# Two half-tile loads of u from a doubled copy in DRAM, with the scan's partitions reordered

## The chip, the cores and the metric

The kernel runs on one core of one Trainium2 chip. The metric is the device time of one execution in microseconds, the median over runs. The profiled execution is one more run of the same program with the hardware profiler on. Its span is the time from the first to the last instruction of the program.

## The reference

The program computes four layers on x of shape (64, 11, 11, 128): 64 images of 121 tokens with 128 channels. Each layer is a mixer (called conv in the names) and then a feed-forward part (a mixture of experts in layer 0, a recurrent net in layers 1 and 2, a spectral filter in layer 3), both with a normalization ahead and a residual sum behind. The change lies in the mixer alone. Cut to what matters, with L = 256 positions (the inner channels are scanned over), D = 121 scan channels (the tokens) and 16 states n:

```python
xz = x @ in_proj_w.T                         # 128 -> 512 per token
xc, z = split(xz)                            # 256 each
xc = silu(conv1d(xc) + conv_b)               # per image: 121 tokens x 256
x_dbl = einsum('bkdl,kcd->bkcl', xs, x_proj_w)   # k = 0, 1: two directions
dts, Bs, Cs = split(x_dbl)                   # 8 ranks, 16 states, 16 states
delta = softplus(einsum('bkrl,kdr->bkdl', dts, dt_proj_w) + dt_proj_b)
dA  = exp(delta[..., None] * A)              # b k d l n
dBu = delta[..., None] * Bs * xs[..., None]  # = u * B, with u = delta * xs
h_l = dA_l * h_(l-1) + dBu_l                 # scan along l, for each b k d n
y   = einsum('bkdln,bknl->bkdl', h, Cs) + Ds * xs
y   = y[:, 0] + flip(y[:, 1])
out = (layernorm(y) * gelu(z)) @ out_proj_w.T
```

For each image b, direction k and scan channel d there is one row delta and one row u of 256 positions. The scan needs each of them once for every one of the 16 states.

## The kernel before

**Tiling.** A mixer works on 8 images at a time (CB = 8, so 8 groups c per layer) and on two directions k, which makes 16 passes m = 2c + k per layer and 64 in the program. The 128 partitions of a pass are 16 states times 8 images, partition = 8 * state + image. A pass walks over the 121 scan channels two at a time, in 61 steps (PAIRS). For every step:

- `rows` (L680, matmul at L686) spreads delta of a channel over the partitions: a 0/1 matrix `pick` (120 x 128, made in `made`, L146 to L150) picks the 8 images' delta, kept as three bf16 parts in the tile R, and repeats it for each state, into a PSUM tile da, five of which go round.
- `exps` (ACT, L699) makes exp(A * delta) in place, with A per partition.
- `scan` (DVE, L707) runs the recurrence over 2 x 256 positions, with da as the factor and ub as the addend, and writes one column of H or HX.
- `by_c` (PE, L728) multiplies blocks of H with C, held in Cz as one column per image (made from `own`, L170, by `own_c` on POOL).

**How u reaches the scan.** `steps` computes delta and u = delta * t for the next pass on PE, ACT and POOL, two images at a time, and `store` (L361 and L362) writes them to DRAM: delta to dD, u to uD of shape [group, direction, image, 128 channels, 256]. `load_u` (L659, the transfer at L663) brings u of four channels (a tile T, 31 tiles per pass, 1984 in all) to all 128 partitions: the source is the 8 images' rows of 4 x 256 floats, repeated for 16 states by a stride of zero. That makes 128 packets of 4 KB, 512 KB per tile. Six buffers (UB) go round. `times_b` (POOL, L675) then multiplies the tile by B in place, and two scans read it.

**What sets the order.** `run` writes every operation under a step number: the table AT (L87) has the step, within a pass or a group, at which each operation is put out, and each engine executes its own instructions in that order. Loads of u stand 10 steps ahead of their first scan (AT "lu"), the multiplication by B 5 steps ahead ("tb"). Loads of R (`load_r`, four quarters of a pass, two buffers) stand at "r0" to "r3". All DMAs of the mixer are issued by one queue, SP's, in order: a DMA that waits for its buffer holds back every DMA behind it. Each of them also waits for the DMA eight places ahead of it, since eight completion semaphores go round.

**Other lines that the change touches.** `load_bc` (L645) loads B and C of a pass to 128 partitions, one row of 1 KB each. `weights` loads A_logs (L135), repeated for the 8 images.

Of the kernel before, what the change touches and what calls it, by code (L numbers as in the profile page):

```python
# [8 lines left out]
F32 = mybir.dt.float32  # L9
# [31 lines left out]
def bcast(ap, n):  # L41

    return ap.unsqueeze(2).to_broadcast([ap.shape[0], ap.shape[1], n])
# [27 lines left out]
def act_tables(nc, which):  # L71
# [13 lines left out]
RING = 5  # L85
UB = 6
AT = {  # L87
    "x": -12.5, "st": -3, "mv": 3, "sc2": 6, "sc3": 8, "nm": 10, "tn": 13.5, "td": 15.5, "tn2": 17.5,
    "td2": 19.5, "cv": 20, "cve": 49, "silu": 52, "p0": 53, "pa0": 3.75, "s0": 66, "b0": 66, "ba0": 7.875,
    "p1": 100, "pa1": 2.25, "s1": 109, "b1": 111, "ba1": 7.5, "u": 4, "d0": 1, "r": 3, "d1": 5, "l": 6.5,  # L90
    "d2": 7, "dst": 12.5, "bc": 54, "bca": 3, "sk": 99, "ska": 2.5, "y0": 15.5, "y1": 35, "y2": 57.5, "y3": 82,
    "k0": 27, "k1": 44.5, "k2": 66.5, "k3": 89, "ka": 2, "ks": 2.5, "km": 4.5, "k2s": 6.5, "k3s": 9, "kn": 11,
    "kg": 13, "xa": 28.5, "xb": 66, "g0": 38, "z0": 77, "g1": 81.5, "z1": 109, "ga": 5, "za": 3.5, "gt": 117.5,
    "gta": 2, "ge": 126.5, "cz": 8, "cza": 3.75, "lbc": -18, "lu": 10, "tb": 5, "ys": 8, "ysa": 1, "ysh": 8,
    "r0": -10, "r1": 2, "r2": 23, "r3": 37,
}


class Conv:
# [9 lines left out]
    def weights(self, setup, fixed, ps):  # L109
        cx, nc, a = self.cx, self.nc, self.cx.a  # L110
        p = f"L{self.l}_conv_"

        def load(pool, name, shape, src):
            t = pool.tile(shape, F32, name=name)
            nc.sync.dma_start(t, src)
            return t

        in_x = load(setup, "in_x", [128, 2, C], a[p + "in_x"].rearrange("(q p) c -> p q c", p=128))
        conv_wT = load(
            setup, "conv_wT", [128, 3, 2, L], a[p + "conv_wT"].rearrange("j (q p) o -> p j q o", p=128)  # L120
        )
        x_dt = load(setup, "x_dt", [8, 2, D], a[p + "x_dt"])
        dt_wT = load(setup, "dt_wT", [8, 2, D], a[p + "dt_wT"])
        self.Ds = fixed.tile([128, 2], F32, name="Ds")
        nc.vector.memset(self.Ds, 0.0)
        nc.sync.dma_start(self.Ds[:D], a[p + "Ds"])
        self.in_zT = load(fixed, "in_zT", [C, L], a[p + "in_zT"])
        self.conv_b = load(fixed, "conv_b", [1, L], a[p + "conv_b"])
        self.x_bc = load(fixed, "x_bc", [D, 4 * NS], a[p + "x_bc"])
        self.norm = load(fixed, "norm", [D, 2], a[p + "norm"])  # L130
        self.out_wT = load(fixed, "out_wT", [128, 2, C], a[p + "out_wT"].rearrange("(q p) c -> p q c", p=128))

        self.A = fixed.tile([128, 2, D], F32, name="A")
        for k in range(2):
            nc.sync.dma_start(self.A[:, k, :], a[p + "A_logs"][k].unsqueeze(1).to_broadcast([NS, CB, D]))  # L135
        return lambda: self.made(setup, fixed, ps, in_x, conv_wT, x_dt, dt_wT)

    def made(self, setup, fixed, ps, in_x, conv_wT, x_dt, dt_wT):
        cx, nc, a = self.cx, self.nc, self.cx.a
        p = f"L{self.l}_conv_"  # L140
        af = self.A.rearrange("p k d -> p (k d)")
        nc.scalar.activation(af, af, AF.Exp)
        nc.vector.tensor_scalar_mul(af, af, -1.0)


        pick = setup.tile([5 * 24, 5, CB], F32, name="pick")  # L146
        nc.vector.reduce_sum(pick, cx.ident[:120, :120].rearrange("p (a s b) -> p a b s", s=3, b=CB), axis=AX.X)
        self.pick = fixed.tile([5 * 24, 5, NS, CB], BF16, name="pick16")
        for i in range(5):
            nc.vector.tensor_copy(self.pick[:, i], pick[:, i, :].unsqueeze(1).to_broadcast([120, NS, CB]))  # L150

        self.w_conv = fixed.tile([C, 3, L], F32, name="w_conv")
        for j in range(3):
            pw = ps.tile([C, L], F32, name="pw", tag="mm")
            for q in range(2):
                nc.tensor.matmul(pw, in_x[:, q, :], conv_wT[:, j, q, :], start=(q == 0), stop=(q == 1))
            nc.scalar.copy(self.w_conv[:, j, :], pw)


        self.w_dt = fixed.tile([D + 1, 2, 128], F32, name="w_dt")  # L160
        nc.vector.memset(self.w_dt, 0.0)
        nc.sync.dma_start(self.w_dt[D : D + 1, :, :D], a[p + "dt_b"].unsqueeze(0))
        for k in range(2):
            pw = ps.tile([D, D], F32, name="pdt", tag="mm")
            nc.tensor.matmul(pw, x_dt[:, k, :], dt_wT[:, k, :], start=True, stop=True)
            nc.scalar.copy(self.w_dt[:D, k, :D], pw)
        self.ones = fixed.tile([1, 128], F32, name="ones")
        nc.vector.memset(self.ones, 1.0)

        self.own = fixed.tile([128, CB], F32, name="own")  # L170
        nc.vector.reduce_sum(self.own, cx.ident.rearrange("p (n b) -> p b n", b=CB), axis=AX.X)

    def buffers(self, fixed, work, ps_f, dram):
        cx, nc, NC = self.cx, self.nc, self.NC
# [12 lines left out]
            nc.gpsimd.memset(x[:, :, 0 : D + 2 : D + 1], 0.0)  # L187
        self.skip = [fixed.tile([D, CB, L], F32, name=f"skip{i}") for i in range(2)]
        self.yst = fixed.tile([128, 64, D], F32, name="yst")
        self.uD = dram.tile([NC, 2, CB, 128, L], F32, name="uD")  # L190
        self.dD = dram.tile([NC, 2, 128, 3, CB, L], BF16, name="dD")
        self.bcD = dram.tile([NC, 4 * NS, CB, L], F32, name="bcD")
        self.yD = dram.tile([NC, L, CB * D], F32, name="yD")
# [99 lines left out]
    def steps(self, c, k, at=None):  # L293
# [10 lines left out]
        for b in range(0, CB, 2):  # L304
# [54 lines left out]

            def store(b=b, s=s):  # L360
                nc.sync.dma_start(self.dD[c, k, :, :, b : b + 2, :].rearrange("d s b l -> d s (b l)"), s["d"])  # L361
                nc.sync.dma_start(  # L362
                    self.uD[c, k, b : b + 2].rearrange("b d l -> d b l"), s["u"].rearrange("p (b l) -> p b l", l=L)
                )

            i = b // 2
            fs = (u, first, rest, second, less, third, store)
# [272 lines left out]
    def load_bc(self, m):  # L640
        c, k = m // 2, m % 2
        for name, at in (("Bt", 0), ("Cp", NS)):
            x = self.work.tile([128, L], F32, name=name, bufs=2)
            r0 = 2 * NS * k + at
            self.nc.sync.dma_start(x, self.bcD[c, r0 : r0 + NS].rearrange("r b l -> (r b) l"))  # L645
            self.bc[m, name] = x

    def own_c(self, m, u):
# [9 lines left out]
    def load_u(self, T):  # L658
        m, i = divmod(T, TILES)  # L659
        n = min(4, D - 4 * i)  # L660
        x = self.work.tile([128, 4, L], F32, name="ub", bufs=UB)
        self.ub[T] = x
        self.nc.sync.dma_start(  # L663
            x[:, :n, :].rearrange("p d l -> p (d l)"),
            self.uD[m // 2, m % 2, :, 4 * i : 4 * i + n, :]
            .rearrange("b d l -> b (d l)")
            .unsqueeze(0)
            .to_broadcast([NS, CB, n * L]),
        )

    def times_b(self, T):
        m, i = divmod(T, TILES)
# [7 lines left out]
    def rows(self, g):  # L680

        m, p = divmod(g, PAIRS)
        for j in range(self.channels(p)):
# [1 line left out]
            n = 24 if d == D - 1 else 120  # L685
            self.nc.tensor.matmul(  # L686
                self.da[g % RING][:, j, 1:],
                self.pick[:n, d % 5].rearrange("p n b -> p (n b)"),
                self.R[m, d // 35][:n, d % 35 // 5, 1:],
                start=True,  # L690
                stop=True,
# [803 lines left out]
```

## Time and profile before

| what | value |
|---|---|
| median of 3 runs | 7753.25 us (7753.02 to 7753.61) |
| the profiled execution | 7752.68 us, span 7750.9 us |
| busy, PE / DVE / ACT / POOL | 6041.0 / 5659.8 / 5449.4 / 5293.3 us |
| POOL, u times B (L675) | 4557.2 us in 1984 instructions of 2323 ns |
| DVE, scans (L707) | 2391.8 + 2130.4 us |
| ACT, exponentials (L699) | 3291.7 us |
| loads of u (ub<-uD) | 1920 of 512 KB and 64 of 128 KB |
| stores of u (uD<-u) | 256 of 256 KB |
| moved by DMA | 1536.54 MB in 905471 packets |

The profile has one line per engine with its busy share in 40 slices of the span, the same for the 16 DMA engines, a list of groups of instructions (busy time, mean of one, idle time ahead of them and what ended it), a list of waits, and the chain of work that ended last. The four mixers can be read off the DMA line: four stretches near 9, with the feed-forward parts between and behind them. A matmul's busy time is modelled, so PE's 78% is not a measure of how full PE is. The shares are averages over stages with different limits, so each stretch is also asked for by itself.

### The profile page before, as it was taken

The page shows a single profiled execution, that of the slowest core. Times are in us where ns is not written, and L with a number is a line of the kernel's source. Part 1 is how long each engine was busy: PE and PEld are TensorE (multiplying, and loading weights), DVE is VectorE, ACT ScalarE, POOL GpSimd, SP SyncE. Part 2 cuts the span into 40 slices and gives each one's busy share as a digit, 9 for nine tenths or more (in the row PEclk, how much of TensorE's full clock was granted, in tenths as well). Part 3 has the DMA queues.
Part 4 walks back from the last instruction along what each step waited for, and adds up shares of the span by engine and source line. Part 5 has one row for each costly group of instructions (what it writes and reads, how often), then busy time and mean ns, then how long its engine had stood idle before and what let it go on. Part 6 is the DMA issues. An engine that isn't in the chain of part 4 may idle for free. (4 is left out here: it accounts for less than half of the span.)

```text
span 7750.9 us, 208787 instructions
## 1 busy us (share of the span) xinstructions
PE 6041.0 (78%) x84334; PEld 3448.5 (44%) x84334; DVE 5659.8 (73%) x7849; ACT 5449.4 (70%) x12343; POOL 5293.3 (68%) x2659
## 2 busy tenths in 40 slices
PE   6788778776788877766788888767678887758999
PEld 3444444465344444444344444434344444434445
DVE  5888888844788888962788888871788888872201
ACT  7888888733888888853788888862788888852200
POOL 6798999812888888931888888940888898960000
PEclk8888898777898989875889989875788888879999
DMA  7899999856899999942899999951899999971111
GB/s 181 227 247 243 245 246 243 215 167 170 221 241 249 246 240 244 247 110 75 220 241 244 246 248 243 243 140 37 217 236 243 243 245 241 245 184 46 35 39 36
DMA packets 905471, 1536.54 MB, mean 198 GB/s; under 512 B 136840, under 2 KB 617442, under 8 KB 904503
## 3 DMA queue, kind: packets, MB, share of 16 engines
q1 hardware_dynamic: 903223, 1521.09, 76.3%
q8 instruction: 662, 10.85, 0.6%
q14 instruction: 306, 2.51, 0.1%
q10 hardware_dynamic: 1280, 2.10, 0.1%
HBM read 1265.98 MB, written 256.97 MB: 196 GB/s over the span
## 5 line engine op out<-in xcount | busy, mean ns | idle before, releaser
L675 POOL TENSOR_TENSOR ub<-ub,Bt 128x1024 f32<-128x1024 f32 (+1 forms) x1984 | 4557.2, 2323 | 589.7 <-DMA ub<-uD 447.1
L699 ACT ACTIVATE da<-da,A 128x255 f32<-128x255 f32 x7744 | 3291.7, 451 | 696.1 <-PE da L686 612.0
L707 DVE TENSOR_TENSOR_SCAN H<-da,ub 128x512 f32<-128x512 f32 x2048 | 2391.8, 1208 | 354.4 <-POOL ub L675 183.9
L707 DVE TENSOR_TENSOR_SCAN HX<-da,ub 128x512 f32<-128x512 f32 (+1 forms) x1856 | 2130.4, 1190 | 318.5 <-POOL ub L675 160.1
L686 PE MATMUL da<-R,pick 120*128 120x255 bf16 x7744 | 1658.9, 305 | 546.0 <-DVE H L707 277.3
L686 PEld LDWEIGHTS <-pick 120*128 120x128 bf16 x7744 | 662.9, 103 | 1494.6 <-issue 1054.9
L728 PE MATMUL yb<-H,Cz 128*16 128x64 f32 x32768 | 782.2, 236 | 187.7 <-ACT yst L745 107.7
L728 PE MATMUL yb<-HX,Cz 128*16 128x64 f32 x32768 | 813.4, 237 | 122.6 <-DVE HX L707 62.7
L728 PEld LDWEIGHTS yb<-HX,Cz 128*16 128x16 f32 x32768 | 531.3, 105 | 641.9 <-issue 338.1
L728 PEld LDWEIGHTS yb<-H,Cz 128*16 128x16 f32 x32768 | 540.9, 103 | 584.0 <-issue 313.3
L263 PE MATMUL pc<-w_conv,xnT 128*121 128x256 f32 x1344 | 458.7, 433 | 27.4 <-ACT d L358 18.6
L184 POOL MEMSET t<- 128x2048 f32 x4 | 7.2, 1805 | 599.6 <-PE px L1221 211.8
L313 PE MATMUL pd<-t,w_dt 122*128 122x512 f32 x480 | 317.6, 749 | 101.7 <-ACT t L274 55.1
L745 ACT COPY yst<-yb 128x512 f32<-128x512 f32 (+2 forms) x640 | 334.9, 551 | 83.9 <-DMA yD<-yst 70.2
L743 DVE TENSOR_TENSOR yst<-yst,yb 128x512 f32<-128x512 f32 (+2 forms) x640 | 337.1, 543 | 73.7 <-PE yb L728 73.2
L340 PE MATMUL pr<-sp,ident 128*128 128x512 f32 x480 | 302.7, 717 | 80.0 <-ACT sp L301 75.0
L333 POOL TENSOR_TENSOR u<-sp,t 128x512 f32<-128x512 f32 x240 | 307.6, 1282 | 33.9 <-DMA uD<-u 32.8
L1294 DVE COPY U<-pu 128x488 f32<-128x488 f32 x128 | 85.4, 667 | 282.5 <-PE pu L1327 282.5
L1296 ACT COPY U<-pu 128x488 f32<-128x488 f32 x128 | 72.9, 570 | 308.7 <-PE pu L1327 308.7
L652 POOL TENSOR_TENSOR Cz<-Cp,own 128x512 f32<-128x512 f32 x256 | 275.5, 1076 | 0.0
L329 ACT CAST d<-sp 128x512 bf16<-128x512 f32 x240 | 148.6, 619 | 172.1 <-DMA dD<-d 171.9
L263 PEld LDWEIGHTS pc<-w_conv,xnT 128*121 128x121 f32 x1344 | 211.7, 194 | 94.9 <-ACT d L358 25.0
(237 smaller groups left out, 7243.8 us busy)
## 6 DMA issues: line engine op xcount, KB each, us to landing
ub<-uD SPq DMA_DIRECT2D x1920, 512.0 KB
dD<-d SPq DMA_DIRECT2D x256, 384.0 KB
R<-dD SPq DMA_DIRECT2D x192, 420.0 KB
uD<-u SPq DMA_DIRECT2D x256, 256.0 KB
yD<-yst SPq DMA_DIRECT2D x512, 60.5 KB
y<-yD SPq DMA_DIRECT2D x112, 242.0 KB
bcD<-bc SPq DMA_DIRECT2D x128, 128.0 KB
w1g<-in_L_ffn_weight_dram SPq DMA_DIRECT2D x16, 1024.0 KB
```

The source lines that it names most:

```text
L263: nc.tensor.matmul(pc, lhs, rhs, start=(j == 0), stop=(j == taps - 1))
L313: nc.tensor.matmul(s["p"], self.w_dt[:, k, :], tb[: D + 1], start=True, stop=True)
L333: nc.gpsimd.tensor_mul(s["u"], s["sp"], tb)
L340: nc.tensor.matmul(s["pr"], self.cx.ident, s["sp"], start=True, stop=False, skip_group_check=True)
L652: self.nc.gpsimd.tensor_mul(self.Cz[u], C.unsqueeze(2).to_broadcast([128, 64, CB]), self.own.unsqueeze(1).to_broadcast([128, 64, CB]),)
L675: self.nc.gpsimd.tensor_mul(x, x, self.bc[m, "Bt"].unsqueeze(1).to_broadcast([128, n, L]))
L686: self.nc.tensor.matmul(self.da[g % RING][:, j, 1:], self.pick[:n, d % 5].rearrange("p n b -> p (n b)"), self.R[m, d // 35][:n, d % 35 // ...
L699: self.nc.scalar.activation(x, x, AF.Exp, scale=self.A[:, m % 2, d : d + 1])
L707: self.nc.vector.tensor_tensor_scan(self.H[dq % 2][:, :n, p - DQ[dq][0]], self.da[g % RING].rearrange("p j l -> p (j l)")[:, :n], x.rearra ...
L728: self.nc.tensor.matmul(self.yb[32 * q : 32 * q + 16, slot % 8, :, :, :w], self.Cz[slot // 8][:, place % 64 : place % 64 + 2, :].rearrange ...
L743: nc.vector.tensor_add(dst, dst, src)
L745: nc.scalar.copy(dst, src)
```

## The change

u is stored twice in DRAM: uD gets a dimension of 2 behind the image, and `store` issues two DMAs with the same data. A tile of u is then loaded by two transfers of 256 KB, one for partitions 0 to 63 and one for 64 to 127. The source of each is 16 rows (image, copy), each repeated for four partitions that follow one another, where it was 8 rows, all repeated 16 times. So that this fits, the partitions stand in another order: half of the states, image, state within the half (partition = 64 * half + 8 * image + state). `pick`, `own`, A and the loads of B and C follow that order; B, C and A are loaded in two halves. Besides that, 18 entries of AT are moved, most of them by half a step to two steps; "r1" goes from 2 to -6, "gt" from 117.5 to 114.5.

```diff
--- before.py
+++ after.py
@@ -85,14 +85,14 @@
 RING = 5
 UB = 6
 AT = {
-    "x": -12.5, "st": -3, "mv": 3, "sc2": 6, "sc3": 8, "nm": 10, "tn": 13.5, "td": 15.5, "tn2": 17.5,
-    "td2": 19.5, "cv": 20, "cve": 49, "silu": 52, "p0": 53, "pa0": 3.75, "s0": 66, "b0": 66, "ba0": 7.875,
-    "p1": 100, "pa1": 2.25, "s1": 109, "b1": 111, "ba1": 7.5, "u": 4, "d0": 1, "r": 3, "d1": 5, "l": 6.5,
-    "d2": 7, "dst": 12.5, "bc": 54, "bca": 3, "sk": 99, "ska": 2.5, "y0": 15.5, "y1": 35, "y2": 57.5, "y3": 82,
-    "k0": 27, "k1": 44.5, "k2": 66.5, "k3": 89, "ka": 2, "ks": 2.5, "km": 4.5, "k2s": 6.5, "k3s": 9, "kn": 11,
-    "kg": 13, "xa": 28.5, "xb": 66, "g0": 38, "z0": 77, "g1": 81.5, "z1": 109, "ga": 5, "za": 3.5, "gt": 117.5,
-    "gta": 2, "ge": 126.5, "cz": 8, "cza": 3.75, "lbc": -18, "lu": 10, "tb": 5, "ys": 8, "ysa": 1, "ysh": 8,
-    "r0": -10, "r1": 2, "r2": 23, "r3": 37,
+    "x": -12.5, "st": -3, "mv": 3, "sc2": 6, "sc3": 8, "nm": 10, "tn": 12.5, "td": 14.5, "tn2": 17.5, "td2": 19.5,
+    "cv": 20, "cve": 49, "silu": 51, "p0": 53, "pa0": 3.75, "s0": 66, "b0": 66, "ba0": 7.875, "p1": 99.5,
+    "pa1": 2.25, "s1": 109, "b1": 111, "ba1": 7.5, "u": 3, "d0": 1, "r": 3, "d1": 4, "l": 6.5, "d2": 7, "dst": 12.5,
+    "bc": 54, "bca": 3, "sk": 99, "ska": 2.5, "y0": 17, "y1": 35, "y2": 56.5, "y3": 82.5, "k0": 26.5, "k1": 44.5,
+    "k2": 65.5, "k3": 89.5, "ka": 2, "ks": 2.5, "km": 4.5, "k2s": 6, "k3s": 9, "kn": 11, "kg": 13, "xa": 30.5,
+    "xb": 66, "g0": 36, "z0": 77, "g1": 81.5, "z1": 109, "ga": 5, "za": 3.5, "gt": 114.5, "gta": 2, "ge": 124.5,
+    "cz": 8, "cza": 3.75, "lbc": -18, "lu": 10, "tb": 5, "ys": 8, "ysa": 1, "ysh": 8, "r0": -10, "r1": -6, "r2": 23,
+    "r3": 37,
 }
 
 
@@ -132,7 +132,9 @@
 
         self.A = fixed.tile([128, 2, D], F32, name="A")
         for k in range(2):
-            nc.sync.dma_start(self.A[:, k, :], a[p + "A_logs"][k].unsqueeze(1).to_broadcast([NS, CB, D]))
+            for h in range(2):
+                A = a[p + "A_logs"][k, 8 * h : 8 * h + 8].unsqueeze(0).to_broadcast([CB, 8, D])
+                nc.sync.dma_start(self.A[64 * h : 64 * h + 64, k, :], A)
         return lambda: self.made(setup, fixed, ps, in_x, conv_wT, x_dt, dt_wT)
 
     def made(self, setup, fixed, ps, in_x, conv_wT, x_dt, dt_wT):
@@ -145,9 +147,10 @@
 
         pick = setup.tile([5 * 24, 5, CB], F32, name="pick")
         nc.vector.reduce_sum(pick, cx.ident[:120, :120].rearrange("p (a s b) -> p a b s", s=3, b=CB), axis=AX.X)
-        self.pick = fixed.tile([5 * 24, 5, NS, CB], BF16, name="pick16")
+        self.pick = fixed.tile([5 * 24, 5, 2, CB, 8], BF16, name="pick16")
         for i in range(5):
-            nc.vector.tensor_copy(self.pick[:, i], pick[:, i, :].unsqueeze(1).to_broadcast([120, NS, CB]))
+            for h in range(2):
+                nc.vector.tensor_copy(self.pick[:, i, h], bcast(pick[:, i, :], 8))
 
         self.w_conv = fixed.tile([C, 3, L], F32, name="w_conv")
         for j in range(3):
@@ -168,7 +171,9 @@
         nc.vector.memset(self.ones, 1.0)
 
         self.own = fixed.tile([128, CB], F32, name="own")
-        nc.vector.reduce_sum(self.own, cx.ident.rearrange("p (n b) -> p b n", b=CB), axis=AX.X)
+        own = setup.tile([128, 2, CB], F32, name="own2")
+        nc.vector.reduce_sum(own, cx.ident.rearrange("p (h b n) -> p h b n", h=2, b=CB), axis=AX.X)
+        nc.vector.tensor_add(self.own, own[:, 0], own[:, 1])
 
     def buffers(self, fixed, work, ps_f, dram):
         cx, nc, NC = self.cx, self.nc, self.NC
@@ -187,7 +192,7 @@
             nc.gpsimd.memset(x[:, :, 0 : D + 2 : D + 1], 0.0)
         self.skip = [fixed.tile([D, CB, L], F32, name=f"skip{i}") for i in range(2)]
         self.yst = fixed.tile([128, 64, D], F32, name="yst")
-        self.uD = dram.tile([NC, 2, CB, 128, L], F32, name="uD")
+        self.uD = dram.tile([NC, 2, CB, 2, 128, L], F32, name="uD")
         self.dD = dram.tile([NC, 2, 128, 3, CB, L], BF16, name="dD")
         self.bcD = dram.tile([NC, 4 * NS, CB, L], F32, name="bcD")
         self.yD = dram.tile([NC, L, CB * D], F32, name="yD")
@@ -359,9 +364,11 @@
 
             def store(b=b, s=s):
                 nc.sync.dma_start(self.dD[c, k, :, :, b : b + 2, :].rearrange("d s b l -> d s (b l)"), s["d"])
-                nc.sync.dma_start(
-                    self.uD[c, k, b : b + 2].rearrange("b d l -> d b l"), s["u"].rearrange("p (b l) -> p b l", l=L)
-                )
+                for i in range(2):
+                    nc.sync.dma_start(
+                        self.uD[c, k, b : b + 2, i].rearrange("b d l -> d b l"),
+                        s["u"].rearrange("p (b l) -> p b l", l=L),
+                    )
 
             i = b // 2
             fs = (u, first, rest, second, less, third, store)
@@ -642,7 +649,9 @@
         for name, at in (("Bt", 0), ("Cp", NS)):
             x = self.work.tile([128, L], F32, name=name, bufs=2)
             r0 = 2 * NS * k + at
-            self.nc.sync.dma_start(x, self.bcD[c, r0 : r0 + NS].rearrange("r b l -> (r b) l"))
+            for h in range(2):
+                rows = self.bcD[c, r0 + 8 * h : r0 + 8 * h + 8]
+                self.nc.sync.dma_start(x[64 * h : 64 * h + 64], rows.rearrange("r b l -> b r l"))
             self.bc[m, name] = x
 
     def own_c(self, m, u):
@@ -660,13 +669,12 @@
         n = min(4, D - 4 * i)
         x = self.work.tile([128, 4, L], F32, name="ub", bufs=UB)
         self.ub[T] = x
-        self.nc.sync.dma_start(
-            x[:, :n, :].rearrange("p d l -> p (d l)"),
-            self.uD[m // 2, m % 2, :, 4 * i : 4 * i + n, :]
-            .rearrange("b d l -> b (d l)")
-            .unsqueeze(0)
-            .to_broadcast([NS, CB, n * L]),
-        )
+        rows = self.uD[m // 2, m % 2, :, :, 4 * i : 4 * i + n, :].rearrange("b i d l -> (b i) (d l)")
+        for h in range(2):
+            self.nc.sync.dma_start(
+                x[64 * h : 64 * h + 64, :n, :].rearrange("p d l -> p (d l)"),
+                rows.unsqueeze(1).to_broadcast([2 * CB, 4, n * L]),
+            )
 
     def times_b(self, T):
         m, i = divmod(T, TILES)
@@ -685,7 +693,7 @@
             n = 24 if d == D - 1 else 120
             self.nc.tensor.matmul(
                 self.da[g % RING][:, j, 1:],
-                self.pick[:n, d % 5].rearrange("p n b -> p (n b)"),
+                self.pick[:n, d % 5].rearrange("p h b n -> p (h b n)"),
                 self.R[m, d // 35][:n, d % 35 // 5, 1:],
                 start=True,
                 stop=True,
```

## The prediction

> **What bounds the kernel now.** I read the page's slices first, then its chain and groups.
>
> ```profile
> DMA  7899999856899999942899999951899999971111
> GB/s 181 227 247 243 245 246 243 215 167 170 221 241 249 246 240 244 247 110 75 220 241 244 246 248 243 243 140 37 217 236 243 243 245 241 245 184 46 35 39 36
> ...
> PE 17%; ACT 7%; DMA 7%; DVE 5%; issue 4%; POOL 3%; SPq 0%; DVEq 0%; ACTq 0%; POOLq 0%
> ...
> L675 POOL TENSOR_TENSOR ub<-ub,Bt 128x1024 f32<-128x1024 f32 (+1 forms) x1984 | 4557.2, 2323 | 589.7 <-DMA ub<-uD 447.1
> ...
> ub<-uD SPq DMA_DIRECT2D x1920, 512.0 KB
> ```
>
> In the mixers the DMA line stands at 9 while the rate sticks near 245 GB/s. POOL, the engine that receives u, was idle 589.7 us ahead of L675, 447.1 of it for the loads of u. Stretches of the third and fourth mixer, a stretch with loads of u alone, and one with plain loads of expert weights:
>
> ```profile
> 3700.00:5150.00 1450.00, 1145.33 (x19660) 643.77 (x19658) 1264.65 (x1554) 1209.89 (x2731) 1267.29 (x628) 0.87 0.94 236
> 5450.00:6900.00 1450.00, 1133.57 (x19279) 635.73 (x19276) 1265.53 (x1558) 1216.81 (x2753) 1282.31 (x638) 0.86 0.94 238
> ...
> 68.00:70.00 2.00, 0.00 (x0) 0.00 (x0) 0.47 (x1) 1.78 (x5) 2.00 (x2) 0.50 1.05 252
> ...
> 1685.00:1687.00 2.00, 2.00 (x11) 2.00 (x11) 0.00 (x0) 0.00 (x0) 0.00 (x0) 0.50 1.05 396
> ```
>
> The columns are PE, PEld, DVE, ACT and POOL busy, clock, DMA share, GB/s. In a mixer POOL is busy 88%, DVE 87%, ACT 84%, and DMA 94%: four resources are nearly full, DMA the most. Yet with all DMA engines busy the loads of u move 252 GB/s and the weights 396. In the trace's packet records a 4 KB packet takes 255 ns on average (255,077 of them) and 159 ns when nothing hinders it (the median of the stores around 5371 us, and 23% of all). The third view is of waits:
>
> ```profile
> POOL ub L675 <- DMA ub<-uD: 447.1, 313, 14.9
> ...
> PEld L686 <- DMA R<-dD: 87.0, 42, 9.9
> ```
>
> and SP's own:
>
> ```profile
> SPq L663 <- DVE H L707: 1730.4, 826, 7.5
> SPq L663 <- DVE HX L707: 1342.3, 635, 6.1
> ```
>
> SP spends 3073 us waiting for scans to free a buffer of u. It has time to issue more.
>
> [...] Before has one transfer of 64 partitions, the store bcD<-bc: its 2 KB packets take 140 ns around 42 us, where the weights' take 84 in the median. [...] this speaks against the change. [...] The load of 121 rows around 1574 us has 11 packets in flight at once[...].
>
> **Why a packet takes 255 ns.** Two causes fit. [...] Shared rows: all 16 engines read the same 4 KB of DRAM at once. Transfers with own rows and blocks of neighbouring partitions show the first alone: the first load of R (62.7 to 65 us) has 36.8 ns against an undisturbed 27 (1.36 times), the loads HX<-mid around 1575 us 201 against 159 (1.27). Loads of u by themselves (65.5 to 76 us) have 269 (1.69). The difference, 1.69 against about 1.31, I put down to shared rows, which the change ends. The first load of conv_b, one row of 1 KB to 121 partitions, shows it too: 61 ns on average against 44 for its undisturbed packets.
>
> **The change part by part.**
>
> Loads of u: 245,760 packets of 4 KB remain. [...] I take 1.31 times 159 = 208. That is 47 ns by 15,360 packets per engine: -722 us of DMA time.
>
> Second store of u: 256 DMAs, 16 packets of 1 KB per engine, 52.3 ns each in the mixers: +214 us. Its issue (580 to 620 ns) is 256 x 0.6 = 154 us of SP.
>
> More DMAs: the two programs have 4207 and 6583, 2376 more (1984 half loads, 256 stores, 128 for B and C, 8 for A). Each ends in a completion packet per engine, 13 ns: +31 us. SP's issue of a load of u is 515 ns, and the 64-row bcD<-bc is no cheaper (480 to 520), so the half loads cost SP 1984 x 0.515 = 1022 us. The 3073 us of buffer waits cover it. Uncovered, a tile would come half a microsecond later, in 313 waits 160 us; but the first half takes 4 x 208 ns = 0.8 us to move, so the second is in its queue in time. Nothing.
>
> Each DMA still waits for the one eight places ahead, which now is four tiles instead of eight. SP waited 34.0 us for that in all; tripled it is 100, under the same cover. [...]
>
> DMA sum: -722 + 214 + 31 = -477 us, of 5617 us that the packets take in the four mixers (16 engines, 6140 us). The share falls from 0.94 to about 0.86.
>
> Moved "r1": the second load of R stands 8 steps earlier, at -6, while the last rows of the pass before still read its buffer until step -4. SP stands for two steps of 1.57 us (6140 us over 3904 steps), 64 times, with loads of u queued behind. Those have five steps (7.9 us) until POOL wants them, and need 3.9 (0.5 to issue, 1.3 to the first packet of a load into idle queues, 2.1 to move). Cost between -50 (R's 87 us of waits shrink) and +190 (cover gone); I take 0. The other entries move the same instructions by at most 3 steps: 0, between -40 and +40. PE, POOL and SP keep their instructions otherwise; DVE and SP have a few more in the setup, behind the feed-forward parts, and 1.3 us ahead of the first mixer.
>
> From DMA time to span: the free share of DMA goes from 6% to 14%, and I take half of POOL's 447.1 us away: -224. POOL's other waits at L675 are 143 of 590, a quarter; they take back 56 as DVE, ACT and PE come due next. R's waits fall in the same moments and are not counted. 7752.7 - 224 + 56 + 1 = 7586; the median stands 0.6 us above the profiled execution, so 7587.
>
> **The rivals.**
>
> Nothing is relieved, and the second store is in the way (the other sign). Place: the queues ahead of POOL's L675, behind each store of u. For it: the bcD<-bc packets at 1.67[...]. Against: R and HX<-mid at 1.27 to 1.36. Price: +245 us of DMA time on a share of 0.94; 50% to 95% reaches the end: 7875 to 7985. It decides where a packet falls by less than 245 / 15,360 = 16 ns, so stays above 239.
>
> Engines in step: [...] packets at 266 to 302. DMA +414 to +967 us, against 370 us free: 8000 to 8650. For it: bcD again; against: in the mixers the loads come ragged, and 23% of the packets already run undisturbed.
>
> Full relief: packets near 170, DMA no longer binds. Against more than that: POOL at 88% would go to 93%. All 447 less a quarter: -335, 7418.
>
> The change may not do what it says: relief of just 16 ns, and gain and store cancel: 7738 to 7768.
>
> **How the numbers follow.** Part relief, 7440 to 7720: 0.50. Full relief: 0.07. Cancelled: 0.07. Second store in the way: 0.27. In step: 0.09. What can be told from no change is 0.2%, 15.5 us. Faster 0.57, same 0.07, slower 0.36. The forecast is the likeliest, 7587, with its own range 7440 to 7720. The range 7400 to 7980 leaves out the in-step case and the edges of two others, under 0.2.
>
> **What would show it.** 4 KB packets near 208 ns; DMA share near 0.86 in the same stretches of a mixer; POOL's wait for ub<-uD near 220 us; R's waits below 153 (87.0 for PEld, 66.0 for PE); written to HBM 67 MB more than 256.97. Wrong if the packet stays above 239, if SP waits for DMAs rather than scans, or if POOL's gain reappears as waits of DVE for ACT.

## The result, and the profile after

| | before | after |
|---|---|---|
| median | 7753.14 us (7744.28 to 7753.61, 4 runs) | 7871.21 us (7863.89 to 7878.85, 4 runs) |
| ratio | | 1.0155, 95% interval 1.0138 to 1.0173 |
| profiled execution, its span | 7752.68, 7750.9 us | 7863.89, 7862.1 us |

The changed kernel is 1.55% slower. The forecast was 7587, faster by 2.1%: its sign is wrong. The time lies in the stated range, just below the band of the rival in which the second store is in the way (7875 to 7985).

The experiments below were each compared with runs of the kernel before made beside them (medians of 7765 to 7769 us), so their ratios do not follow from 7753.

From the page of the changed kernel: the DMA slices, what went through memory, POOL's product and the two issues.

```profile
DMA  7899999956899999942899999960899999971111
GB/s 187 230 251 253 252 253 251 229 151 174 230 257 254 254 248 253 252 119 69 224 250 250 251 251 249 250 163 22 220 245 251 253 252 257 250 198 47 35 39 36
...
HBM read 1265.98 MB, written 324.08 MB: 202 GB/s over the span
...
L683 POOL TENSOR_TENSOR ub<-ub,Bt 128x1024 f32<-128x1024 f32 (+1 forms) x1984 | 4560.0, 2323 | 701.6 <-DMA ub<-uD 580.3
...
ub<-uD SPq DMA_DIRECT2D x3840, 256.0 KB
uD<-u SPq DMA_DIRECT2D x512, 256.0 KB
```

The 67 MB more that are written are the second copy of u. DMA moves some 8 GB/s more in the mixers, and its slices still stand at 9. The same two stretches as before (PE, PEld, DVE, ACT and POOL busy, clock, DMA share, GB/s):

```profile
3700.00:5150.00 1450.00, 1120.96 (x18542) 619.00 (x18556) 1225.25 (x1505) 1193.04 (x2690) 1240.61 (x616) 0.85 0.94 246
5450.00:6900.00 1450.00, 1105.53 (x17951) 615.87 (x17964) 1200.24 (x1495) 1173.55 (x2630) 1202.03 (x602) 0.87 0.91 241
```

The share is 0.94 and 0.91 where 0.86 was forecast, at a rate 4% and 1% higher. POOL does less in the same 1450 us (616 and 602 pieces of work where it did 628 and 638). The waits of those who receive u and R:

```profile
POOL ub L683 <- DMA ub<-uD: 580.3, 354, 19.9
...
PEld L694 <- DMA R<-dD: 107.9, 44, 11.8
...
PE da L694 <- DMA R<-dD: 75.9, 27, 10.2
```

All three grew: POOL's from 447.1 us, R's from 87.0 and 66.0. The last of these, and SP's wait for DMAs at the loads of u, in the kernel before:

```profile
PE da L686 <- DMA R<-dD: 66.0, 28, 8.3
...
SPq L663 <- DMA ub<-uD: 34.0, 46, 2.4
```

SP's own waits at the loads of u (L674) in the changed kernel:

```profile
SPq L674 <- DVE H L715: 613.5, 372, 6.6
SPq L674 <- DVE HX L715: 529.7, 393, 6.8
...
SPq L674 <- DMA ub<-uD: 339.8, 721, 1.7
...
SPq L674 <- DMA R<-dD: 115.4, 76, 3.5
```

SP waited 3073 us for scans before and waits 1143 now. The DMA landings in the traces of both kernels fall on eight semaphores, and SP's waits for the DMA eight places ahead, a load of u or of R, rose from 34.0 us to 455 here. The prediction had named as a sign of being wrong "if SP waits for DMAs rather than scans"; this goes that way, though scans are still the larger part.

For the comparisons below I worked out one table from the trace's packet records and issues. It takes, in each of the four mixers, the stretch from the last issue of the 20th tile's load to the first of the 477th's, of 496, and adds the four up. "Busy" is the time of all packets divided by 16 engines, "idle" is the rest, both in us. The packet column is the mean of the packets of 4096 bytes that start in the stretches. "Late" is the mean time from the end of the scan that frees a tile's buffer to the end of the last issue of that tile's load.

| kernel | transfers per tile | ratio to before | stretch | busy | idle | 4 KB packet, ns | late, us |
|---|---|---|---|---|---|---|---|
| before | 1 | 1 | 5440 | 5137 | 303 | 255.6 | 1.37 |
| after | 2 | 1.0155 | 5536 | 5251 | 284 | 247.9 | 3.37 |
| e1_store | 1 | 1.0100 | 5516 | 5294 | 223 | 253.5 | 1.76 |
| h1_halves | 2 | 1.0077 | 5494 | 5126 | 367 | 251.8 | 3.00 |
| e2_oldat | 2 | 1.0199 | 5588 | 5305 | 283 | 252.2 | 3.39 |
| e4_one | 1 | 1.0045 | 5458 | 5141 | 317 | 246.2 | 1.58 |
| s3_row | 2 | 1.0055 | 5490 | 5201 | 289 | 258.1 | 2.13 |
| s4_row | 3 | 1.0280 | 5661 | 5256 | 405 | 262.2 | 3.82 |
| s1_tiny | 2 | 1.0084 | 5513 | 5220 | 293 | 257.2 | 2.24 |
| s2_tiny | 3 | 1.0392 | 5769 | 5330 | 438 | 262.2 | 4.45 |
| v1_middle | 3 | 1.0345 | 5699 | 4867 | 831 | 238.3 | 5.77 |

In the last column the s-kernels are measured at the load of u, with their extra transfers behind it.

### The profile page after: what moved, and what is told of

The parts are those of the page before. It is cut to its first block, busy times and chain, and to the rows that moved or that the text cites. A ratio compares the mean times of both kernels' runs of the same rounds, so it can differ in the third digit from the quotient of the medians.

```text
span 7862.1 us, 214588 instructions
## 1 busy us (share of the span) xinstructions
PE 6067.6 (77%) x84282; PEld 3442.9 (44%) x84334; DVE 5671.2 (72%) x7873; ACT 5442.1 (69%) x12343; POOL 5293.6 (67%) x2659
## 5 line engine op out<-in xcount | busy, mean ns | idle before, releaser
L683 POOL TENSOR_TENSOR ub<-ub,Bt 128x1024 f32<-128x1024 f32 (+1 forms) x1984 | 4560.0, 2323 | 701.6 <-DMA ub<-uD 580.3
```

The lines of the kernel that those rows point to most:

```text
L683: self.nc.gpsimd.tensor_mul(x, x, self.bc[m, "Bt"].unsqueeze(1).to_broadcast([128, n, L]))
```

## The experiments

### Which partitions, or shared rows

A program of loads alone, none of the mixers: 30 loads one after the other in each of six forms, from a DRAM tensor laid out like uD (the comments number the forms). "Shared" are 8 rows (4 in form 6), all repeated 16 times, "own" are 16 rows, each repeated for 4 or 8 partitions that follow one another.

```diff
+    def before(t, i):                       # form 1: 8 rows, repeated 16 times
+        nc.sync.dma_start(t, shared(i, 128, 8))
+    def halves(t, i):                       # form 2: 16 own rows, twice 64 partitions
+        for h in range(2):
+            nc.sync.dma_start(t[64 * h : 64 * h + 64], own(i, 4))
+    def one(t, i):                          # form 3: 16 own rows, 128 partitions
+        nc.sync.dma_start(t, own(i, 8))
+    def middle(t, i):                       # form 4
+        nc.sync.dma_start(t[32:96], own(i, 4))
+    def low(t, i):                          # form 5
+        nc.sync.dma_start(t[0:64], own(i, 4))
+    def middle_shared(t, i):                # form 6: 4 rows, repeated 16 times
+        nc.sync.dma_start(t[32:96], shared(i, 64, 4))
```

> No mixer is in this kernel: it copies x to the output and then loads 4 KB rows of a small DRAM buffer in six forms, 30 buffers each, nothing else moving. The forms: (a) as before, 16 copies of 8 shared rows; (b) as after, two halves of 16 own rows by 4 partitions; (c) one transfer of 16 own rows by 8 partitions; (d) 16 own rows by 4 partitions to partitions 32 to 95 alone; (e) the same to partitions 0 to 63 alone; (f) partitions 32 to 95 with 16 copies of 4 shared rows. Theory of shared rows (the prediction's): the mean 4 KB packet is near 269 ns in (a), near 208 in (b) and (c), and (f) is slower than (d). [...] (a), (b) and (c) are all between 255 and 285 ns, (d) is near 159 and (e) near 300 although both have own rows, and (f) equals (d).

The windows of the six forms in that order (the last two columns are DMA share and GB/s):

```profile
64.00:107.00 43.00, 3.23 (x21) 0.00 (x0) 1.00 1.03 251
133.00:179.00 46.00, 3.25 (x22) 0.00 (x0) 1.00 1.04 243
203.00:246.00 43.00, 2.99 (x20) 0.00 (x0) 1.00 1.03 235
270.00:287.00 17.00, 5.96 (x42) 0.00 (x0) 1.00 0.94 331
300.00:327.00 27.00, 3.07 (x21) 0.00 (x0) 1.00 1.03 204
342.00:359.00 17.00, 6.34 (x44) 0.00 (x0) 1.00 0.96 342
```

In these windows packets of 4 KB take 267 ns in the form of before, 275 in that of the change and 285 in one transfer of own rows: rows of their own bring nothing. Sixty-four partitions from 32 to 95 take 183.3 ns with own rows and 181.9 with shared ones, with a median of 159, the undisturbed time. From 0 to 63 it is 327, with a median of 326. So which partitions are written decides between these (331 and 342 GB/s against 204), and not whether rows are shared. The prediction's step on 255 ns had put the length down to shared rows; here it does not come from them. Why the packets of the three forms with 128 partitions take 267 to 285 ns, no run shows.

### The second store alone

```diff
-        self.uD = dram.tile([NC, 2, CB, 128, L], F32, name="uD")
+        self.uD = dram.tile([NC, 2, CB, 2, 128, L], F32, name="uD")
...
-                nc.sync.dma_start(
-                    self.uD[c, k, b : b + 2].rearrange("b d l -> d b l"), s["u"].rearrange("p (b l) -> p b l", l=L)
-                )
+                for i in range(2):
+                    nc.sync.dma_start(
+                        self.uD[c, k, b : b + 2, i].rearrange("b d l -> d b l"),
+                        s["u"].rearrange("p (b l) -> p b l", l=L),
+                    )
```

> The kernel before with u stored twice and the second copy never read; everything else as before. Theory of the second store: the 214 us of DMA time that it adds reach the end by more than half, 7860 to 7960 us. Theory that the halves cost it (their issues, completions and the waits on eight semaphores): the store is hidden, 7750 to 7790 us.

Measured: 7844.55 us, 1.0100 (1.0080 to 1.0119), nearer to the first theory and just under its band. In the table it adds 157 us of busy time: packets of 1 to 2 KB, which hold the stores of u, add 177 for 92% of the added stores, and those of 4 KB give back 28. Idle time takes up 80, and the stretch is 76 us longer. POOL's wait, and the third mixer:

```profile
POOL ub L677 <- DMA ub<-uD: 540.5, 341, 15.8
```

```profile
3700.00:5150.00 1450.00, 1122.39 (x18813) 625.98 (x18813) 1240.85 (x1531) 1207.58 (x2725) 1259.10 (x627) 0.86 0.96 249
```

DMA goes to a share of 0.96, in this window and over the four stretches (5294 of 5516 us), and of the engine time added beside the loads of u about half is paid. That supports the first view of the prediction: DMA is what binds. The 256 stores also take 256 issues and places in SP's queue, which this run does not separate; by the cost of transfers of a single number further below (1984 for 0.55%) they would be worth some 6 of the 77 us, an estimate that takes a store to hold its place no longer than such a transfer does.

### The halves without the store, and one transfer without the halves

The changed kernel with one store of u; the rows of this pass and of the one before stand for the two copies, so half of the states scan the u of another pass, while the number and size of the loads stay (the first pass of each mixer still stores twice, 16 stores in all):

```diff
-        self.uD = dram.tile([NC, 2, CB, 2, 128, L], F32, name="uD")
+        self.uD = dram.tile([2 * NC + 1, CB, 128, L], F32, name="uD")
...
-        rows = self.uD[m // 2, m % 2, :, :, 4 * i : 4 * i + n, :].rearrange("b i d l -> (b i) (d l)")
+        rows = self.uD[m : m + 2, :, 4 * i : 4 * i + n, :].rearrange("m b d l -> (m b) (d l)")
```

> The kernel after without the second store: the 16 rows of a half are 8 of the pass before and 8 of this pass, so half of the states scan the wrong u and the values are not the reference's, while loads, partitions and order are those of the kernel after. Theory of the second store: without its 214 us of DMA time the kernel is at 7700 to 7770 us. Theory of the halves' own cost: it stays at 7820 to 7870 us.

Measured: 7810.43 us, 1.0063 (1.0043 to 1.0082), and POOL's wait for ub is 512.2 us. The time lies between the bands of the two theories. The store of the changed kernel is therefore worth about 0.9%, much as on the kernel before, and the halves do not pay even when it is left out.

The changed kernel with one transfer of 16 own rows, eight partitions from each, so that partitions are ordered images, states:

```diff
-        for h in range(2):
-            self.nc.sync.dma_start(
-                x[64 * h : 64 * h + 64, :n, :].rearrange("p d l -> p (d l)"),
-                rows.unsqueeze(1).to_broadcast([2 * CB, 4, n * L]),
-            )
+        self.nc.sync.dma_start(
+            x[:, :n, :].rearrange("p d l -> p (d l)"), rows.unsqueeze(1).to_broadcast([2 * CB, 8, n * L])
+        )
```

> The kernel after with one transfer per tile in place of two halves: 16 own rows by 8 partitions each, partitions ordered by images, then states; u is still stored twice, and the moved entries of AT stay. Theory of shared rows: a packet of 4 KB falls to about 208 ns on its own rows and the time is below that of the kernel before, 7600 to 7720 us. [...] the packet stays at 245 to 260 ns, and the second store is left: 7840 to 7920 us. Theory of the halves' own cost: 7750 to 7800 us.

Measured: 7798.63 us, 1.0045 (1.0030 to 1.0061). Store, rows and table of places are those of the changed kernel; the division in halves is gone (with it go the split loads of B and C, and the partitions stand as images, states), and 1.1% of the time. POOL waits 85 us less for u than in the changed kernel (580.3):

```profile
POOL ub L674 <- DMA ub<-uD: 495.5, 314, 19.3
```

The 4 KB packets are nearly as long as in the changed kernel (246.2 ns against 247.9). What the halves add in the table is nonetheless busy time, 110 us (68 in packets under 1 KB, 27 in completions, 26 in packets of 4 KB, less 13 in those of 1 to 2 KB), while idle time falls by 33. Own rows in this order are 9 ns shorter in the mixers than shared ones (255.6), and with the same two stores this kernel is faster than e1_store (1.0045 against 1.0100; its new table by itself did nothing for the kernel before, as the next section shows). So a part of the relief came, a fifth of the forecast 47 ns; why it came here and not in the program of loads stays unexplained.

### The table of places

The changed kernel with the old AT (the last lines of the table are shown, for this one alone), and the kernel before with the new one:

```diff
-    "cz": 8, "cza": 3.75, "lbc": -18, "lu": 10, "tb": 5, "ys": 8, "ysa": 1, "ysh": 8, "r0": -10, "r1": -6, "r2": 23,
-    "r3": 37,
+    "gta": 2, "ge": 126.5, "cz": 8, "cza": 3.75, "lbc": -18, "lu": 10, "tb": 5, "ys": 8, "ysa": 1, "ysh": 8,
+    "r0": -10, "r1": 2, "r2": 23, "r3": 37,
```

> The kernel after with the table AT of the kernel before, so only the transfers, the second store and the order of partitions are changed. The runs so far leave the halves at about +1% if the moved entries gain about 0.5%, and at about +0.5% if they do nothing. If the moved entries help: slower than the kernel after, 7890 to 7930 us. If they do nothing: 7860 to 7880. If they hurt, above all r1 with its early wait on SP: 7800 to 7850.

> The kernel before with only the 18 moved entries of AT. If they help by themselves: 7710 to 7740 us. If they fit only the halves: 7750 to 7800.

Measured: 7921.32 us, 1.0199 (1.0179 to 1.0220), and 7764.38 us, 0.9999 (0.9986 to 1.0011). The new table is worth 0.4% to the changed kernel and nothing to the one before. With the old table the waits for R are 145.5 and 117.2 us, with the new one 107.9 and 75.9: R's second quarter, issued eight steps earlier, may gain where SP's queue runs late. Which of the 18 entries does it was not tried.

### Halves alone

The same kernel as without the store, with the old table:

> Halves alone: the changed kernel with the old table of places and one store of u (the rows of this pass and of the pass before stand in for the two copies, so half the states scan a wrong u). Sum of parts: the changed kernel with the old table less the second store on the kernel before, 1.0199 - 1.0100 = 0.010, so 1.008 to 1.012. If store and halves make each other worse, less: 1.003 to 1.007.

Measured: 7826.43 us, 1.0077 (1.0058 to 1.0096). With the store alone (1.0100) the sum is 1.0177, and both together with the old table gave 1.0199, which the intervals don't tell from the sum. In the table busy time is as it was (5126 against 5137): the 4 KB packets save 55 us and those of 1 to 2 KB 15, and the completion packets (+24 us) and the packets under 1 KB (+33 us, 42.0 ns in place of 39.8) take most of it back. What grew is idle time, by 65 us, for a stretch that is 54 us longer. From e1_store to e2_oldat, halves on top of the store, it is +60 of idle and +11 of busy. Both pairs change two things, though: the rows become own ones, which saves busy time (153 us from e1_store to e4_one, one transfer each), and the transfer is divided. Against the single transfer of own rows, above, the division alone showed as busy time. So the table does not tell whether the halves lose by idle engines or by longer packets. What goes with them in every pair is lateness: here 3.00 us in the mean against 1.37.

### Three parts over the middle partitions

The program of loads suggested partitions 32 to 95 for the first four images, with the others on both sides, one store of u and the old table, then the new one:

```diff
+PARTS = ((32, 0, 4), (0, 4, 2), (96, 6, 2))
...
+        for p0, b0, nb in PARTS:
+            self.nc.sync.dma_start(
+                x[p0 : p0 + NS * nb, :n, :].rearrange("p d l -> p (d l)"),
+                self.uD[m // 2, m % 2, b0 : b0 + nb, 4 * i : 4 * i + n, :]
...
+                .to_broadcast([NS, nb, n * L]),
+            )
```

> The kernel before, u stored once, with a tile loaded by three transfers: 16 copies of images 0 to 3 to partitions 32 to 95, 16 copies of images 4 and 5 to partitions 0 to 31, and of 6 and 7 to 96 to 127; pick, own, A, B and C follow. [...] the middle's packets run at 159 ns as in form (d), the other half's at up to 320, a mean near 220, which is 15360 x 34 ns = 520 us less DMA time; POOL's wait for u falls and the time with it, 7500 to 7680 us. Theory that the halves' own cost grows with the number of transfers (issues, and waits on the eighth DMA ahead): three transfers cost more than two and eat the gain, 7750 to 7900 us.

> The same three transfers with the 18 moved entries of AT. If the moved entries help wherever the loads are in several parts: 20 to 40 us below v1_middle. If not: within 15 us of it.

Measured: 8025.69 us, 1.0345 (1.0329 to 1.0360), and 8054.37 us, 1.0376 (1.0359 to 1.0393). Both lie above every expectation, and the new table does not help here. The packets did become the shortest of the table, 238.3 ns, and busy time fell by 270 us, half of what was expected. Idle time rose by 529. SP's waits in the first of the two, and its third mixer:

```profile
SPq L674 <- DVE H L718: 194.6, 216, 4.9
...
SPq L674 <- DMA ub<-uD: 120.1, 297, 1.8
SPq L674 <- DVE HX L718: 111.3, 109, 3.9
```

```profile
3700.00:5150.00 1450.00, 1104.29 (x17276) 618.76 (x17275) 1155.59 (x1443) 1135.16 (x2551) 1148.88 (x574) 0.85 0.82 220
```

With DMA at 0.82 of its time and POOL at 0.79, neither is full. SP's 3073 us of waits for scans are down to 306: its queue has 5952 loads of u to issue, at a median of 590 ns, 3512 us. What more issues cost is what the next experiments test on the kernel before.

### An extra transfer with next to no bytes

Behind each load of u in the kernel before, one or two transfers that nothing reads, of 16 numbers, and then of a single number (the diff is of two, with 16 numbers):

```diff
+        for h in range(2):
+            j = (2 * T + h) % 8
+            self.nc.sync.dma_start(self.ex[:, j : j + 1], self.uD[m // 2, m % 2, h, 0:16, 0:1])
```

> The kernel before, and behind each load of u one more transfer on the same queue, of 16 numbers of 4 bytes each, which nothing reads: 1,984 transfers with next to no bytes. Theory 'issues' (halved loads cost time because SP's queue has twice as many transfers to issue, about 515 ns each, and twice as many places in the row of eight): the ratio to before is 1.007 to 1.013, as the halves cost (the changed kernel over the one with a single transfer of own rows: 1.0155 - 1.0045 = 0.011); SP's waits on the scans fall from 3073 us to 1200 to 2100, POOL's wait for ub rises above 500 us. Rival 'bytes and ports' (the halves cost time by how their packets meet at the engines or because the later half lands late): ratio 0.998 to 1.003, POOL's wait stays within 40 us of before.

> The same with two such transfers behind each load. 'Issues': as the loads in three parts over the middle partitions lost, without their gain in packets: 1.025 to 1.045, SP's waits on the scans under 600 us. 'Bytes and ports': 0.998 to 1.005.

> The kernel before, and behind each load of u one transfer of a single number (one packet and one completion on one engine, in place of 16 and 16). It takes an issue and a place in the row of eight as before, but next to none of the engines' time. 'Issues and places': 1.005 to 1.010, as with 16 rows (1.0084). 'Packets' (the 16 small packets and 16 completions, 46 us of each engine's time by the trace, cost that time): 0.998 to 1.003.

> The same with two such transfers behind each load. 'Issues and places': 1.03 to 1.04, as with 16 rows (1.0392). 'Packets': 1.000 to 1.008.

Measured, with 16 numbers: 1.0084 (1.0069 to 1.0099) for one and 1.0392 (1.0377 to 1.0408) for two. With a single number: 1.0055 (1.0039 to 1.0071) and 1.0280 (1.0253 to 1.0306). SP's waits of the kernel with one single number (L664 is the load of u, L673 the extra transfer):

```profile
SPq L664 <- DVE HX L711: 856.9, 508, 4.9
SPq L664 <- DVE H L711: 830.0, 501, 6.7
...
SPq L673 <- DMA ub<-uD: 276.1, 247, 2.6
...
SPq L664 <- DMA ub<-uD: 253.1, 243, 2.8
```

and with two:

```profile
SPq L673 <- DMA ub<-uD: 856.6, 791, 3.4
SPq L664 <- DMA ub<-uD: 532.4, 448, 4.1
...
SPq L664 <- DVE H L711: 260.2, 215, 5.5
SPq L664 <- DVE HX L711: 205.7, 186, 3.8
```

Two thirds of the cost stay when 15 of the 16 numbers go (0.55 of 0.84, 2.80 of 3.92), and the packets with them. The issues get shorter too (a median of 437 ns in place of 586 for one, 250 in place of 421 for two), so the third that goes is not packets alone. Most of what such a transfer costs here thus comes from its issue and from its holding one of eight places. The waits say more of which: SP's waits for the load of u eight places ahead rise from 34 us to 529 and 1389 at these two lines, and the waits for scans fall from 3073 to 1687 and 466. The 3968 extra issues of the last kernel take a median of 250 ns, 1.0 ms in all, as much as the halves add (1984 at 529 ns), and cost 2.8% where the halves cost 0.8%. With three transfers to a tile, eight places hold fewer than three tiles. This points to the place as the dearer part there; no run changes the number of places, and for the halves, at two to a tile, issue and place weren't separated.

With one extra number the loss appears as busy time (5201 us against 5137, 4 KB packets of 258.1 ns), not as idle engines (289 us, 303 before), as it does for the halves against a single transfer of own rows. The ranges of one extra number and of the halves alone overlap (1.0039 to 1.0071, 1.0058 to 1.0096), so a second transfer for each tile can cost about as much as the halves do without dividing the load. How late issues lengthen packets isn't shown.

### Fewer transfers

One load for two tiles, in the form of before and in the three parts. Buffers are three of double size, loads are due 8 steps ahead and products 4:

```diff
-UB = 6
+UB = 3
...
+        if i % 2:
+            return
+        n = min(8, D - 4 * i)
+        x = self.work.tile([128, 8, L], F32, name="ub", bufs=UB)
+        self.ub[T] = x[:, :4]
+        if n > 4:
+            self.ub[T + 1] = x[:, 4:]
```

> The kernel before, with one load for two tiles (8 channels, 8 KB for each partition) into three buffers of twice the size; loads are due 8 steps ahead in place of 10, products 4 in place of 5, because a buffer comes free only when both its tiles are scanned. Half the issues. 'Issues': before has issues to spare (its SP waits 3073 us), so fewer gain nothing, and the coarser buffers cost: ratio 1.005 to 1.04. If the issues bound the kernel before as well: 0.985 to 0.995.

> Three transfers for two tiles, images 0 to 3 to partitions 32 to 95, the others to the outer ones: the short packets of the three-part loads at half their issues (1.5 for a tile in place of 3). 'Issues': better than three parts for each tile by 1.5 to 3 %, so 1.00 to 1.02; below 1.00 only if the coarser buffers cost less than the faster packets give. If three parts lost for another reason than their number: 1.03 or above.

Measured: 8366.86 us, 1.0771 (1.0753 to 1.0789), and 8257.96 us, 1.0636 (1.0620 to 1.0652). Both are worse than expected, because the coarse buffers, with the shorter lead that they need, cost far more than I had put on them: POOL waits 1087.1 and 1001.7 us for u, and SP in the first waits over 4 ms for scans:

```profile
SPq L667 <- DVE H L711: 2329.9, 465, 12.0
SPq L667 <- DVE HX L711: 1817.4, 384, 11.1
```

Between the two, the middle partitions gain 1.3%, with fewer issues in the queue. No run has such loads with more or finer buffers, so whether they would beat the kernel before is open.

### Order of the partitions without a second copy

The single transfer of own rows, with the store of before: images ahead of states, each of 8 rows repeated 16 times. With the new table, then the old (the diff is against the single transfer of own rows, and its store and rows are not shown):

```diff
-            x[:, :n, :].rearrange("p d l -> p (d l)"), rows.unsqueeze(1).to_broadcast([2 * CB, 8, n * L])
+            x[:, :n, :].rearrange("p d l -> p (d l)"), rows.unsqueeze(1).to_broadcast([CB, NS, n * L])
```

> One transfer of 128 partitions and one store of u, as in the kernel before, with partitions ordered images, states (an image's row goes to 16 neighbouring partitions[...]), and the new table of places. It is the kernel with a single transfer of own rows (1.0045) without its second store. 'Own rows or their order save packet time, and the second store costs it': 1.0045 - 0.0100 = 0.994 to 0.997, packets near 247 ns. 'Engines that read the same row in step get in each other's way, the part of the shared-row theory that was left for the mixers': packets at 256 ns as before, 0.999 to 1.002.

> The same with the old table of places. The new table did nothing for the kernel before (0.9999) and 0.0044 for the changed one; if it is fitted to two stores and two transfers alone, this is equal to or faster than the run with the new table: 0.990 to 0.997. If packets stay at 256 ns: 0.998 to 1.002.

Measured: 8713.27 us, 1.1212 (1.1190 to 1.1234), and 8771.31 us, 1.1300 (1.1268 to 1.1333). Neither expectation had seen this. From the page of the first:

```profile
DMA  4666666645566666650566666651566666653111
GB/s 163 201 200 211 206 206 208 211 135 183 190 209 210 209 209 205 209 174 30 193 209 210 211 204 203 212 187 35 174 199 210 205 208 212 207 204 88 33 39 36
```

The rate sticks at about 209 GB/s with DMA only six tenths busy. In the packet records of the first mixer most often 8 packets of 4 KB are in flight at a time, where the kernel before most often has 16, and most take the undisturbed 159 ns (mean 178.7). Eight packets of 4096 bytes in 159 ns make 206 GB/s. The outermost dimension has 8 rows, as many as there are packets in flight. The small packets fit this: the page counts 119880 under 512 B, the kernel before 136840. That is 16960 fewer, 8 for each of the 2120 transfers that here have 8 rows outermost (1984 loads of u, 128 of B and C, 8 of A). With 16 own rows in the same order of partitions, in e4_one, the DMA slices stand at 9 and the rate at some 257 GB/s:

```profile
DMA  7899999846899999942899999950899999971111
GB/s 185 231 253 257 257 259 253 229 150 178 229 258 258 258 256 254 256 116 68 225 254 256 256 257 256 254 148 32 219 248 254 254 263 256 255 187 46 35 39 36
```

That is what the second copy of u is for in the order images, states: 16 rows outermost. The question that these two runs were to answer, rows or order, they leave open, since half as many packets are in flight.

## Why the prediction was wrong

**What bounds the kernel: right, within limits.** DMA time added (the second store) is paid for about half: 76 us for 157. But DMA time taken away is worth nothing where the engines are not kept fed: three parts took 270 us off, added 529 of idle and lost 3.45%. The prediction took DMA's share for the one lever, and did not ask what feeds DMA.

**Why a packet takes 255 ns: the step that failed first.** The difference of 1.69 and 1.31 was put down to shared rows. That all 16 engines read one row at once was my assumption: the packet records do not tell which row a packet reads. The program of loads shows no loss from shared rows: 181.9 ns with them and 183.3 without. What decides there is which partitions are written (159 ns in the median for 32 to 95, 326 for 0 to 63). In the mixers the packet went from 255.6 to 247.9 ns, not to 208; of the forecast 722 us, some 54 to 110 came (14,200 packets per engine in the stretches, shorter by 3.8 ns from the kernel before to h1_halves and by 7.7 to the changed kernel). This term alone carried the forecast's sign. The one transfer of 64 partitions in the kernel before, bcD<-bc, spoke against the change, with 140 ns where the weights' packets take 84; I gave it less weight than a ratio taken from loads of another form. In the program of loads the two halves reached 243 GB/s where the lower one alone had 204, 19% more, and still no more than the one transfer of before (251).

**Second store: right in size.** Forecast +214 us of DMA time, measured 177 in 92% of the stores, some 192 in all. Alone it costs 1.0%, some two thirds of the whole. The rival "second store in the way" named this mechanism, and its point of decision, a packet above 239 ns, came true. Its price was too high for the store (77 us where it had 122 to 233) and left out the halves' own cost, so that the measured time came close to its band is luck.

**Completions: right.** +31 us forecast, 26.5 in the stretches of the changed kernel (35,840 more packets of 4 bytes in its trace, 13 ns each in the first mixer).

**"Uncovered ... Nothing": the second step that failed.** The 1022 us of issues were put under 3073 us of SP's waits for scans. That cover is a sum over 1984 tiles, and is not there when it is wanted: in the kernel before half of the loads start 0.06 us after their buffer comes free, but one in ten over 3.3 us after. Those late ones have no waits ahead of them to give up, and what is put into the queue makes them later: with the halves alone one in ten starts over 5.4 us after. The halves alone cost 0.8%, 1.0 to 1.1% on top of the store, and one number more for each tile 0.55%.

**The DMA eight places ahead: the third.** "Tripled it is 100": it is 455 us at the loads of u, in place of 34. Two transfers to a tile leave room for four tiles, and with R and the stores between them for fewer.

**The table of places: taken at 0 between -50 and +190.** It measured 0 on the kernel before and -0.44%, about -34 us, on the changed kernel.

**From DMA time to span.** Half of POOL's 447 us was to go; instead 133 us were added. The sum as it should have been, in shares of the time before: +1.0% store, +0.8% halves, and together with the old table +2.0%, -0.4% table: +1.55%.

**The other rivals.** "Engines in step", 266 ns (1.67 times 159, by bcD<-bc) to 302 (the median of the 4 KB packets of before from 62.7 to 65 us), did not come in the mixers: 247.9. In the program of loads it did (275 for the halves), but there the form of before is as slow (267), so it is no loss against it.

## What to carry to other kernels

A queue's waits for free buffers were no reserve to be spent at will here (3073 us of them, and one load in ten over 3.3 us late): look at how late its latest issues are, not at the sum of its waits, before more transfers are put into it. Where the number of transfers in flight is fixed, as at eight here, one that is cut in two needs two places, so the reach ahead in tiles falls by half, whatever the bytes (SP's waits for those places: 34.0 us before, 455 after). And a cause for slow packets should be tried on the load's own form with one thing changed (other partitions, own or shared rows), before a kernel is built on a ratio between loads of different form.

## What the runs showed of the hardware

- Sixty-four partitions from 32 to 95 were written at 331 to 342 GB/s, and from 0 to 63 at 204, with the same 64 packets of 4 KB: 159 ns against 326 in the median (m1_loads).
- A load of 64 partitions, 32 to 95, took as long for a packet with 4 DRAM rows, all repeated 16 times, as with 16 rows, each for four partitions: 181.9 and 183.3 ns (m1_loads).
- The load of u with 8 rows outermost had most often 8 packets in flight and ended at 209 GB/s, which cost this kernel 12% of its time (o1_order).
- A transfer of a single 4-byte number for each tile, 1984 of them, cost this kernel 0.55%, some 43 us (s3_row), and 3968 of them 2.8%, some 215 us (s4_row).
